# Constant products in TensorE's planned gaps, lower reckoned costs of TensorE, and one PSUM bank for transpositions

## The chip, the cores and the metric

The kernel runs on one core of a Trainium2 chip. The metric is the time of the whole program on the device, in microseconds, and a kernel is judged by the median of several runs. The engines are named as in the profile: PE is TensorE (PEld its weight loads), DVE is VectorE, ACT is ScalarE, POOL is GpSimd and SP is SyncE.

## The reference

Sixteen graphs of 1024 nodes with 64 features each go through four layers. Every layer begins with a layer norm and a ReLU, and its result is added to `x`.

```python
h = jnp.maximum(_layernorm(x, axis=-1), 0.0)
x = x + _L0_gnn_ref(h, adj, L0_gnn_W)     # (adj @ h) @ W.T
...
x = x + _L1_gnn_ref(h, adj, ...)          # two dense layers, adj @ m, a GRU cell
...
x = x + _L2_gnn_ref(h, adj, ...)          # T0 = h, T1 = adj @ h, T2 = 2 adj @ T1 - T0, mixed by K
...
x = x + _L3_gnn_ref(h, adj, nodemask, ...)  # quantiles over thinned lists of neighbours, two dense layers
```

So the first three layers hold four products of a graph's 1024 x 1024 adjacency with 64 columns. The last one lists each node's neighbours, drops some of them by rank, takes three quantiles over the neighbours' rows for every feature, and puts the weighted sum through two dense layers. The adjacency has some nine entries in a row.

## The kernel before

**One program for all graphs.** A graph's nodes lie in 8 tiles of 128. The Python code holds several generators, and each yields one instruction at a time:

- `transposing` loads 128 columns of the adjacency at a time (`block`, 512 KB), transposes them by PE, four 128x128 pieces into one PSUM bank, and lets ACT copy each full bank into half of an `AT` tile. There are 15 `AT` tiles; a graph needs 8 and holds them from its first product with the adjacency to its last.
- `coding` takes the sign of each `AT` tile on ACT (`there`) and multiplies it by powers of two on PE (fp16), so that neighbours are packed in words; `lists` unpacks these on DVE into the neighbours' numbers.
- `layering` runs twice (even and odd graphs) and computes the first three layers in `layers`. Four times per graph a step multiplies the 8 tiles of `h` by the 8 `AT` tiles, two halves of 512 columns each (64 product instructions per graph). Between them are small products by weights, transpositions, and the norms on ACT and DVE. At its end it stores the rows that the last layer gathers (`table`).
- `gathering` waits for a graph's `table` and issues 80 indirect gathers on POOL (10 neighbours of 8 tiles); `quantiling` sorts the gathered rows on DVE by a network of minima and maxima; `dense` sums the weighted places on PE and applies the two dense layers. Nodes with more than 10 neighbours are done once more at the end, in four groups.

**The order.** `Weave` decides the order of all instructions while the program is built. It keeps a reckoned time for each engine. At every step each generator offers its next instruction; the earliest start among the engines wins, and within 0.1 us the lower key (older graph, earlier stage). `Line.cost` (line 309 on) gives each instruction's cost by its engine and shape; `ready` adds 0.15 us for a hand-over between engines. The instructions of one engine are then bound to that order (`behind`), so each engine runs its own queue in order and waits on semaphores for data alone. Costs that are wrong change no result, only the order.

**PSUM.** There are eight banks. Two (`tp`) are for the transpositions of the adjacency, one (`bits`) for coding, two (`q`) for the last layer's dense part and three (`fm`) for the layers. A bank is taken with `yield "tp"` (line 877) and given back after ACT's copy (line 881). Bank 0 is also used by one small product at the end of the program (line 1350).

**The leash.** `issue` can make one engine's instructions wait for another engine's. The two engines are set with `weave.leash`, and they are None and None (line 572): no wait is added.

In the profile nearly all compute instructions carry line 303, that of the helper that records them, so groups are told apart by tiles: `bank<-AT,nodes` is a product with the adjacency, `bank<-c,block` a transposition of it, `bank<-c,there` the coding, `bank<-G,c` the sum over sorted places.

Of the kernel before, what the change touches and what calls it, by code (L numbers as in the profile page):

```python
# [22 lines left out]
P = 128  # L23
# [79 lines left out]
RANK = 3.0  # L103
SHARE = 3
LONGEST = 512
AT = 15
XTILES = 2
PAYS = 3
# [71 lines left out]
def network(n, places, beam=200):  # L180
# [4 lines left out]
    for layer in needed(batcher(n), range(places)):  # L185
        new = {}
        for buf, (cost, ops) in states.items():
            classes = {}
            for a, b, la, lb in layer:
# [73 lines left out]
class Op:  # L263
# [5 lines left out]
    def __init__(self, line, make, writes, reads, cost, later=0.0, after=()):  # L269
        self.line, self.make, self.cost, self.later, self.after = line, make, cost, later, after  # L270
        self.writes, self.reads = [place(a) for a in writes], [place(a) for a in reads]
# [16 lines left out]
class Line:  # L288
# [17 lines left out]
    def cost(self, method, out, reads, kwargs):  # L306
        if method == "dma_start":
            return 0.4, 2.0 + out.nbytes() / 150e3
        n = max(a.free_size() for a in [out] + reads)
        extra = "accum_out" in kwargs  # L310
        if self.name == "DVE":
            fixed = {"match_replace": 0.145, "max": 0.155}.get(method, 0.155)
            return fixed + n / 960 + 0.08 * extra, 0.0
        if self.name == "ACT":
            scalars = sum(hasattr(kwargs.get(k), "ap") for k in ("bias", "scale"))
            return 0.225 + n / 1400 + 0.09 * scalars + 0.19 * extra, 0.0
        if self.name == "PE":
            if method == "transpose":
                return 0.19, 0.25
            n = out.free_size()  # L320
            if n == NB and mybir.dt.size(reads[0].dtype) == 2:
                return 0.075, 0.3
            pair = n == 512 and reads[0].shape[0] == P and out.shape[0] == C
            return (0.58 if pair else max(0.34, 0.06 + n / 545)), 0.3
        return 1.33, 2.2


class Weave:
# [6 lines left out]
    def __init__(self, tc):  # L335
        self.tc = tc
        self.free, self.past, self.last, self.stocks, self.chains = {}, {}, {}, {}, []
        self.ends, self.time, self.free_pairs, self.count = {}, 0.0, set(), 0
        self.leash = None
        self.awaited, self.made = [], {}  # L340

    def stock(self, name, tiles):
        self.stocks[name] = list(tiles)
# [1 line left out]
    def give(self, name, t):  # L345
        self.stocks[name].append(t)
# [10 lines left out]
                        t = max(t, end + (0.0 if line is op.line else 0.15))  # L357
        return t

    def of_others(self, op, line):  # L360

        found = []
        for mine, kinds in ((op.reads, "w"), (op.writes, "wr")):
            for name, lo, hi, p0, p1 in mine:
                for (l, h, q0, q1, kind, other), made in self.made.get(name, {}).items():
                    if other is line and kind in kinds and l < hi and lo < h and q0 < p1 and p0 < q1:
                        found.append(made)
        return [max(found, key=lambda f: f[:2])] if found else []

    def note(self, op, start, ins):  # L370
        end = start + op.cost
        self.count += 1
        for mine, kind in ((op.reads, "r"), (op.writes, "w")):
            for name, lo, hi, p0, p1 in mine:
                past, made = self.past.setdefault(name, {}), self.made.setdefault(name, {})
                if kind == "w":
                    for e in [e for e in past if lo <= e[0] and e[1] <= hi and p0 <= e[2] and e[3] <= p1]:
                        del past[e], made[e]
                past[lo, hi, p0, p1, kind, op.line] = end + op.later
                made[lo, hi, p0, p1, kind, op.line] = end, self.count, ins  # L380

    def advance(self, chain):

# [23 lines left out]

    def issue(self, op, start, of):

        line, ins = op.line, op.make()  # L410
        if line is self.leash[0]:


            done = [i for end, _, i in self.awaited if end <= start]
            self.awaited = self.awaited[len(done):]
            if done:
                self.after(ins, done[-1])
        self.free[line] = start + op.cost
        self.time = max(self.time, start + op.cost)
        if line is not self.leash[1]:  # L420
            self.awaited = sorted(self.awaited + self.of_others(op, self.leash[1]), key=lambda a: a[:2])
        self.note(op, start, ins)
        self.ends[ins.ins.name] = start + op.cost + op.later
        free = False
        for other in self.last.get(line, ()):
            self.behind(ins, other)
        if line in self.last:
            free = (ins.ins.name, self.last[line][0].ins.name) in self.free_pairs
        self.last[line] = [ins] + (self.last[line] if free else [])
        return ins  # L430

    def run(self):
        while True:
            before = None
            while before != (before := [(id(c["want"]), id(c["op"])) for c in self.chains]):
                for chain in sorted(self.chains, key=lambda c: c["key"]):
                    if not self.advance(chain):
                        self.chains.remove(chain)
            heads = [c for c in self.chains if c["op"]]
            if not heads:  # L440
                break
            best = {}
            for c in heads:
                op = c["op"]
                c["start"] = max(self.free.get(op.line, 0.0), op.ready)
                best[op.line] = min(best.get(op.line, 1e9), c["start"])
            line = min(best, key=best.get)
            chain = min((c for c in heads if c["op"].line is line and c["start"] <= best[line] + SLACK),
                        key=lambda c: c["key"])
            op, start = chain["op"], chain["start"]  # L450
            chain["op"], chain["value"] = None, self.issue(op, start, (chain["gen"].__name__, chain["key"]))
        assert not self.chains, [c["want"] for c in self.chains]
# [15 lines left out]
class Fast:  # L468
# [4 lines left out]
    def __init__(self, tc, half, whole, weights):  # L473
        self.tc, self.nc = tc, tc.nc
        (W0, W1, b1, W2, b2, Wih, bih, Whh, bhh, Wc, K, bc, M1, mb1, M2, mb2) = weights
        nc = self.nc
# [7 lines left out]
        _, at16, _, at32 = fast_constants()  # L484
# [84 lines left out]
        self.G, self.D = Line("POOL", nc.gpsimd), Line("SP", nc.sync)  # L569
        self.A = self.S  # L570
        self.take = {}
        weave.leash = None, None

        def stock(name, count, shape, dtype=F32):
            weave.stock(name, [p.tile(shape, dtype, name=f"{name}{i}") for i in range(count)])

        banks = [ps.tile([P, 512], F32, name=f"bank{i}") for i in range(8)]
        self.bank = banks[0]
        weave.stock("tp", banks[0:2])
        weave.stock("bits", banks[2:3])  # L580
        weave.stock("q", banks[3:5])
        weave.stock("fm", banks[5:8])
# [10 lines left out]
        stock("block", 2, [P, NT, P])  # L593
        stock("AT", AT, [P, N])
        stock("X", XTILES, [P, NT, C])
# [183 lines left out]
    def longest(self):  # L779
# [5 lines left out]
        for _ in range(3):  # L785
            tiles.append((yield "AT"))
        run = tiles[0][:, 0:BINS * Q]
# [59 lines left out]
        for t in tiled:  # L847
            self.weave.give("AT", t)


    def transposing(self, adj):
# [17 lines left out]
        for i in range(total):  # L869
# [4 lines left out]
            block = blocks.pop(i)  # L874
            at = yield "AT"
            for half in range(2):
# [39 lines left out]
    def layers(self, w, b, x):  # L916
# [9 lines left out]
        def into(bank, h, last=False):  # L926

            def step(j):
# [6 lines left out]
                if last:  # L935
                    yield lambda: self.masked[b] > j
                    give("AT", turned[j])
            return step
# [208 lines left out]
    def quantiles(self, c):  # L1147
# [21 lines left out]

        few = max(1, int(LONGEST / (T * C)))  # L1170

# [342 lines left out]
def general_layers(tc, b, x, adj, nodemask, VT, mB, X, H, maskT, c16, ident, ones16, ones_row, eps,  # L1514
# [3 lines left out]
    with tc.tile_pool(name="g1", bufs=1) as p1, tc.tile_pool(name="g2", bufs=2) as p2, \  # L1518
# [16 lines left out]
        def neighbours(g):  # L1535
            AT = p2.tile([P, NT, N], F32, name="AT")
            CN = p1.tile([P, NT, N], F16, name="CN")
# [434 lines left out]
```

## Time and profile before

| what | value |
|---|---|
| three runs | 2184.63, 2185.75, 2197.86 us; median 2185.75 |
| profiled execution, its own time | 2165.2 us |
| its span, first to last instruction | 2163.3 us |
| mean granted TensorE clock | 0.785 |
| busy time of PE, DVE, ACT, POOL | 1616.2, 1607.7, 1066.9, 1429.7 us |
| transpositions of the adjacency, mean of one | 345 ns |
| ACT's copies of them (256) | 150.6 us, 591 ns each |
| HBM | 120.12 MB read, 19.17 MB written |

The three layers of all graphs are done after about 1811 us; what is left then is the gathering, sorting and dense part of the last graphs, and the groups of nodes with many neighbours. In the 40 slices of the page a digit is the busy share of an engine in a slice of 54 us, in tenths, and PEclk the clock granted to TensorE in tenths of the full one. In a line of stretches, each engine's busy time is followed by its number of instructions, and the last three numbers are the granted clock, the DMA share and GB/s. A float32 product stands in the records as two matmuls, a transposition as one. PE's matmuls are pipelined, so that their records overlap.

### The profile page before, as it was taken

Reading aid. Unit: us, or ns where it says so; the run is one execution under the profiler, and the core shown is the slowest. Engines: PE = TensorE matmul, PEld = TensorE weight load, DVE = VectorE, ACT = ScalarE, POOL = GpSimd, SP = SyncE. Lnnn points to the kernel's source line nnn. Section 1 sums busy time; section 2 is a strip of 40 time slices with the busy share of each in tenths; the row PEclk is TensorE's granted clock in tenths of the full one; section 3 lists DMA queues with packets and bytes.
Section 4 is the critical chain, followed back from the end, with each engine's and each line's share of the span. In section 5 each row is a group of like instructions: output and inputs, shape, how many; then the busy total and the mean of one; then the engine's idle time right before and its main releaser. Section 6 shows DMA issues by size and latency. Waiting matters only on the chain. (4 is left out here: it accounts for less than half of the span.)

```text
span 2163.3 us, 24623 instructions
## 1 busy us (share of the span) xinstructions
PE 1616.2 (75%) x7024; PEld 745.6 (34%) x7024; DVE 1607.7 (74%) x4253; ACT 1066.9 (49%) x2905; POOL 1429.7 (66%) x1441
## 2 busy tenths in 40 slices
PE   6878787889888987988887978887978865243303
PEld 3433433334333433443433343433334322121302
DVE  1381487787787887869797868787877799959746
ACT  3554655555666456554757475656566632011000
POOL 2027677757576767767576777676767677776772
PEclk9978787797889698869798789889688876555555
DMA  4242525233334234242425242425242213121110
GB/s 120 69 91 47 105 46 95 60 72 77 59 96 66 66 67 95 50 89 56 100 55 100 49 95 61 93 60 105 51 73 70 41 30 43 32 31 22 33 27 11
DMA packets 246846, 141.04 MB, mean 65 GB/s; under 512 B 76048, under 2 KB 223952, under 8 KB 246704
## 3 DMA queue, kind: packets, MB, share of 16 engines
q1 hardware_dynamic: 195664, 88.11, 17.0%
q0 software_dynamic: 46096, 48.62, 14.7%
q10 hardware_dynamic: 4944, 2.67, 0.5%
q8 instruction: 59, 0.97, 0.2%
q14 instruction: 83, 0.68, 0.1%
HBM read 120.12 MB, written 19.17 MB: 64 GB/s over the span
## 5 line engine op out<-in xcount | busy, mean ns | idle before, releaser
L626 POOL DMA_INDIRECT G<-table,pay x1402 | 1400.0, 999 | 687.2 <-issue 358.1
L303 PE MATMUL bank<-AT,nodes 128*64 128x512 f32 x2048 | 588.6, 671 | 87.7 <-ACT nodes L303 73.1
L303 PEld LDWEIGHTS bank<-AT,nodes 128*64 128x64 f32 x2048 | 155.7, 152 | 391.2 <-issue 231.7
L303 PE MATMUL bank<-c,block 128*128 128x128 f32 x976 | 229.4, 345 | 64.8 <-ACT AT L303 40.3
L303 PE MATMUL bank<-G,c 128*128 128x512 f32 (+3 forms) x382 | 175.8, 592 | 130.4 <-DVE G L303 123.0
L303 PEld LDWEIGHTS bank<-c,block 128*128 128x128 f32 x976 | 146.3, 174 | 230.6 <-issue 153.2
L303 ACT ACTIVATE AT<-bank 128x512 f32<-128x512 f32 x256 | 150.6, 591 | 139.9 <-PE bank L303 136.7
L303 DVE TENSOR_TENSOR G<-G 128x512 f32<-128x512 f32 (+3 forms) x313 | 198.3, 677 | 2.3
L303 ACT ACTIVATE wide<-bank 64x512 f32<-64x512 f32 x128 | 75.3, 589 | 164.6 <-PE bank L303 163.4
L303 ACT ACTIVATE sq<-X,st 128x64 f32<-128x64 f32 x360 | 125.4, 348 | 62.0 <-DVE st L303 42.7
L303 ACT ACTIVATE nodes<-X,off,ri 128x64 f32<-128x64 f32 x360 | 143.4, 434 | 23.4 <-DVE off L303 22.6
L303 DVE TENSOR_TENSOR net<-G 128x512 f32<-128x512 f32 (+6 forms) x240 | 151.0, 674 | 4.4 <-ACT G L303 2.7
L303 ACT ACTIVATE G<-G,coef 128x64 f32<-128x64 f32 x384 | 98.9, 341 | 103.2 <-DVE coef L303 103.2
L303 PEld LDWEIGHTS bank<-G,c 128*128 128x128 f32 x382 | 70.1, 227 | 188.9 <-issue 105.8
L303 ACT ACTIVATE there<-AT 128x1024 f16<-128x1024 f32 x128 | 132.3, 1050 | 0.8
L303 PE MATMUL bank<-wide,wg 64*64 64x512 f32 (+1 forms) x192 | 114.7, 687 | 5.9 <-ACT wide L303 5.4
L303 DVE TENSOR_TENSOR G<-net 128x512 f32<-128x512 f32 (+7 forms) x189 | 116.9, 672 | 0.8
L303 DVE TENSOR_TENSOR G<-G,net 128x512 f32<-128x512 f32 (+3 forms) x177 | 110.4, 672 | 0.8
L303 DVE SCALAR_TENSOR_TENSOR G<-bad,G 128x512 f32<-128x512 f32 (+1 forms) x176 | 110.4, 695 | 0.0
L303 DVE RECIPROCAL ri<-sd 128x8 f32<-128x8 f32 x64 | 12.8, 200 | 120.6 <-ACT sd L303 120.4
L303 DVE MAX8 L<-cand 128x8 f16<-128x103 f16 x384 | 92.1, 263 | 8.6
L303 DVE TENSOR_TENSOR net<-G,net 128x512 f32<-128x512 f32 (+3 forms) x140 | 88.2, 670 | 0.1
(199 smaller groups left out, 2359.3 us busy)
## 6 DMA issues: line engine op xcount, KB each, us to landing
block<-in_adj SPq DMA_DIRECT2D x121, 512.0 KB, 4.2
G<-table,pay POOLq DMA_INDIRECT x1402
rows<-pay SPq DMA_DIRECT2D x16, 632.0 KB, 8.8
table<-pay SPq DMA_DIRECT2D x16, 264.0 KB, 4.2
X<-in_x SPq DMA_DIRECT2D x16, 256.0 KB, 8.0
out<-yo SPq DMA_DIRECT2D x16, 256.0 KB, 2.6
G<-in_adj SPq DMA_DIRECT2D x3, 512.0 KB, 9.1
G<-in_adj ACTq DMA_DIRECT2D x3, 512.0 KB, 10.7
```

The source lines that it names most:

```text
L303: return Op(self, lambda: f(*args, **kwargs), writes, reads, cost, later)
L626: return self.nc.gpsimd.indirect_dma_start(out=out, out_offset=None, in_=table, in_offset=bass.IndirectOffsetOnAxis(ap=at, axis=0))
```

## The change

Four things change, in the planner and in the banks.

1. `Line.cost` reckons PE's instructions lower: a transposition 0.125 us (was 0.19), an fp16 product of 64 columns 0.05 (was 0.075), a product with half an `AT` tile 0.27 (was 0.58), any other max(0.15, 0.06 + n/1100) (was max(0.34, 0.06 + n/545)).
2. `fill` is called before every PE instruction. Where the planned start lies more than 0.22 us after the end of PE's last one, and a `layering` generator still lives, it issues products of a constant tile with itself (`ones16`, fp16, 128 rows, 512 columns) into a bank that nobody reads. Their number is such that the planned work of PE in the last 3.4 us comes to half of it, and takes at most 0.7 of the gap. These products have no cost in the plan, and wait for nothing but their place in the queue.
3. Bank 0 becomes the bank of these products. The transpositions keep one bank, `banks[1:2]`.
4. The leash is taken out with its records.

```diff
+WINDOW = 3.4
+DENSITY = 0.5
+SPARE = 0.7
+FILL = 0.22
...
             if method == "transpose":
-                return 0.19, 0.25
+                return 0.125, 0.25
             n = out.free_size()
             if n == NB and mybir.dt.size(reads[0].dtype) == 2:
-                return 0.075, 0.3
+                return 0.05, 0.3
             pair = n == 512 and reads[0].shape[0] == P and out.shape[0] == C
-            return (0.58 if pair else max(0.34, 0.06 + n / 545)), 0.3
+            return (0.27 if pair else max(0.15, 0.06 + n / 1100)), 0.3
...
-        line, ins = op.line, op.make()
-        if line is self.leash[0]:
-
-
-            done = [i for end, _, i in self.awaited if end <= start]
-            self.awaited = self.awaited[len(done):]
-            if done:
-                self.after(ins, done[-1])
+        line = op.line
+        if line is self.filled:
+            self.fill(start, op.cost)
+        ins = op.make()
...
+    def fill(self, start, cost):
+
+        line = self.filled
+        gap = start - self.free.get(line, 0.0)
+        self.recent = [(a, c) for a, c in self.recent if a > start - WINDOW]
+        if gap > FILL and any(c["gen"].__name__ == "layering" for c in self.chains):
+            lacking = DENSITY * WINDOW - sum(c for _, c in self.recent)
+            for _ in range(int(min(lacking, SPARE * gap) / FILL)):
+                ins = self.filler()
+                for other in self.last.get(line, ()):
+                    self.behind(ins, other)
+                self.last[line] = [ins]
+                self.recent.append((start, FILL))
+        self.recent.append((start, cost))
...
-        weave.leash = None, None
+        weave.filled = self.T
...
-        self.bank = banks[0]
-        weave.stock("tp", banks[0:2])
+        self.bank = spare = banks[0]
+        weave.filler = lambda: nc.tensor.matmul(spare, self.ones16[:, 0:P], self.ones16, start=True, stop=True)
+        weave.stock("tp", banks[1:2])
```

More of the change, by code (lines that the diff above doesn't have):

```diff
@@ L337, in __init__ @@
         self.free, self.past, self.last, self.stocks, self.chains = {}, {}, {}, {}, []
-        self.ends, self.time, self.free_pairs, self.count = {}, 0.0, set(), 0
-        self.leash = None
-        self.awaited, self.made = [], {}
+        self.ends, self.time, self.free_pairs = {}, 0.0, set()
+        self.filled, self.recent = None, []
     def stock(self, name, tiles):
@@ L358, in ready, with note @@
         return t
[L360 to L370, printed above, removed]
+    def note(self, op, start):
         end = start + op.cost
-        self.count += 1
         for mine, kind in ((op.reads, "r"), (op.writes, "w")):
             for name, lo, hi, p0, p1 in mine:
-                past, made = self.past.setdefault(name, {}), self.made.setdefault(name, {})
+                past = self.past.setdefault(name, {})
                 if kind == "w":
                     for e in [e for e in past if lo <= e[0] and e[1] <= hi and p0 <= e[2] and e[3] <= p1]:
-                        del past[e], made[e]
+                        del past[e]
                 past[lo, hi, p0, p1, kind, op.line] = end + op.later
-                made[lo, hi, p0, p1, kind, op.line] = end, self.count, ins
     def advance(self, chain):
@@ L408, in issue @@
     def issue(self, op, start, of):
-        line, ins = op.line, op.make()
-        if line is self.leash[0]:
-            done = [i for end, _, i in self.awaited if end <= start]
-            self.awaited = self.awaited[len(done):]
-            if done:
-                self.after(ins, done[-1])
+        line = op.line
+        if line is self.filled:
+            self.fill(start, op.cost)
+        ins = op.make()
         self.free[line] = start + op.cost
         self.time = max(self.time, start + op.cost)
-        if line is not self.leash[1]:
-            self.awaited = sorted(self.awaited + self.of_others(op, self.leash[1]), key=lambda a: a[:2])
-        self.note(op, start, ins)
+        self.note(op, start)
         self.ends[ins.ins.name] = start + op.cost + op.later
```

## The prediction

> **What bounds the kernel now.** I read the page first, then POOL's rows in order of time, then the stretches between one graph's result and the next, then PE's rows in one such stretch.
>
> From the page: engine totals, the granted clock in 40 slices, and the group of gathers.
> ```profile
> PE 1616.2 (75%) x7024; PEld 745.6 (34%) x7024; DVE 1607.7 (74%) x4253; ACT 1066.9 (49%) x2905; POOL 1429.7 (66%) x1441
> ...
> PE   6878787889888987988887978887978865243303
> ...
> PEclk9978787797889698869798789889688876555555
> ...
> L626 POOL DMA_INDIRECT G<-table,pay x1402 | 1400.0, 999 | 687.2 <-issue 358.1
> ```
> No engine is full by this. But a gather takes 0.95 to 1.4 us and POOL needs another 0.30 us ("issue") before the next, so 80 gathers of a graph take 103.9 us on average (100.3 to 107.6, first start to last end of each graph in POOL's rows). The first gather starts at 141.3 us and that of graph 15 at 1819.8: 15 periods of 111.9 us. The 8 us between are POOL waiting for the next graph's table, as in its timeline at the change from graph 6 to graph 7:
> ```profile
> 797.56 0.95 POOL L626 DMA_INDIRECT G<-table,pay  x1 [0.30 <-issue]
> 798.81 0.95 POOL L626 DMA_INDIRECT G<-table,pay  x1 [0.31 <-issue]
> 812.14 0.94 POOL L626 DMA_INDIRECT G<-table,pay  x1 [12.38 <-DVE L L303]
> ```
> The wait is 12.4 us there; all such waits between graphs sum to 121 us. The DVE named is long done: the table of graph 7 was stored at 807.6. So the layers set the period and POOL comes next, 8 us behind. The layers of two graphs hardly overlap: a graph holds its 8 AT tiles from its first aggregation to its last, and there are 15, so the eighth tile of graph b+1 is transposed only when graph b gives its first one back. In the trace graph b+1's first aggregation is added 13 to 22 us after graph b's last. A period is therefore the latency of one graph's chain.
>
> Stretches from one graph's last addition of X to the next one's (length, then busy time and count of PE, PEld, DVE, ACT, POOL, then the clock):
> ```profile
> 340.00:459.50 119.50, 99.36 (x387) 44.59 (x384) 90.34 (x242) 64.92 (x179) 90.30 (x92) 0.74 0.37 72
> 459.50:574.60 115.10, 98.11 (x447) 44.22 (x447) 92.88 (x248) 70.98 (x200) 78.91 (x80) 0.83 0.36 75
> 574.60:684.10 109.50, 94.22 (x416) 41.04 (x415) 89.67 (x242) 67.51 (x189) 74.02 (x76) 0.89 0.35 71
> 684.10:798.90 114.80, 101.16 (x428) 46.46 (x427) 89.20 (x240) 64.96 (x174) 82.98 (x87) 0.78 0.39 80
> ```
> Where the clock is lower, the period is longer. Over the 12 periods from 340 to 1701 us a line through length and clock falls 7.1 us per 0.1 of clock (correlation -0.76). Following the waits back through single periods says the same: PE holds 26 to 27 us of the chain in periods of 108.5 and 109.5 us, and 41 to 69 us in those of 115 to 119.5.
>
> The clock has two values in the records, 1.0 and 0.5, and changes at multiples of 3.41 us; up to 1730 us it is at 0.5 for a third of the time. Two stretches at one value each, and PE's rows there:
> ```profile
> 744.00:762.40 18.40, 18.40 (x58) 10.02 (x56) 11.80 (x23) 5.91 (x10) 13.91 (x15) 0.50 0.22 49
> 784.00:798.90 14.90, 14.59 (x90) 6.61 (x87) 14.78 (x30) 4.26 (x7) 11.24 (x13) 1.00 0.38 62
> ```
> ```profile
> 686.72 0.64 PE L303 MATMUL bank<-c,there 128*128 128x64 f16 x16
> 702.85 0.69 PE L303 MATMUL bank<-c,block 128*128 128x128 f32 x2 [4.58 <-ACT AT L303]
> 713.51 1.97 PE L303 MATMUL bank<-wide,w 64*64 64x512 f32 x2
> 735.44 1.02 PE L303 MATMUL bank<-wide,wg 128*128 128x512 f32 x2
> 785.62 3.65 PE L303 MATMUL bank<-AT,nodes 128*64 128x512 f32 x16 [0.32 <-DVE nodes L303]
> ```
> One f32 product of 512 columns stands as two records: 1.02 us at clock 1.0, 1.97 at 0.5. Eight paired products with AT take 3.65 us at 1.0, 0.46 each. The 4.58 us gap ahead of 702.85 is what the change aims at: behind it PE stays at 0.5 for over 20 us, though it then works nearly without a pause.
>
> **The change, part by part.**
> The leash was set to None, None: it added no wait, so its removal costs nothing and uncovers nothing.
>
> Clock. The new matmuls stand in planned gaps, so that PE is reckoned busy half of any 3.4 us. Real gaps lie only partly where planned ones do, so I take three fifths of the low time as cured: 0.826 becomes about 0.93 in the layers, and by the line above the period falls by 0.104 x 71 = 7.4 us. Ends: 0, if the clock does not rise, and 12.3 (0.174 x 71), if it is 1.0 throughout; beyond 7.7 (111.9 less 104.2: 103.9 and one pause of 0.3) POOL takes over as the bound.
>
> The Trainium skill bears on this ("TensorE: Matmul & The Clock Gate", Part 1: The HAM clock gate): it gives half and full clock and a window of 3.4 us, which agrees with the records here. The same page ("A second HAM failure mode: psum-queue depth-cycling") speaks against the change's one bank: PE that pauses between groups for a bank swings between both clocks. By that rule this part would be 0 and the sum +4 a period, +60 us in all; by the rows it is -7.4 a period.
>
> Fillers. A filler is one f16 product of 512 columns. No such row with 128 rows exists. 16 f16 products of 64 columns, twice as many columns, take 0.64 us at 1.0, so half of that is an upper end, 0.32; the steps inside that run are 29 ns, eight times that is 0.23, the value I take at 1.0, and 0.46 at 0.5. Its number: per graph the new plan reckons 64 x 0.27 + 96 transpositions x 0.125 + 64 x 0.05 + 32 x 0.15 + 8 x 0.18 + 25 x 0.525 + 2 x 0.29 = 52 us of PE (100 us by the old figures), and a plan period is at least 80 x 1.33 = 106 us. PE is thus reckoned 49% busy, and only windows below half are filled: nothing if it were spread evenly, a quarter of the time (27 us) if each window were full or empty. I take 9 us, 40 fillers a graph, some 600 in all. They have no semaphore to wait for; they cost where PE's queue is late and the gap is gone. Behind a filler wait the next product and whatever ACT and DVE do with it. A third on the chain gives +3 us a period; ends 0 and 18 (40 x 0.46, all on the chain). What hides the rest is PE waiting for ACT and DVE.
>
> One bank. A graph has 16 half tiles: four transpositions, then a copy by ACT of 0.59 us (256 copies, 150.6 us). With two banks PE transposes the next half beside the copy; now it starts after it. On the chain is the one tile that graph b+1 lacks, whose second half comes later by about one copy and two handovers, +1 us; ends 0 and 9.4 (16 x 0.59). The other 15 halves have most of a period. The queues behind are PE's, where a transposition that waits for ACT holds the products after it, and ACT's, which has the norm of the layers behind the copy. The DMA of `block` (median landing 4.2 us) waits for the later release, but its tiles lie ahead by up to 7.
>
> Order. PE is now reckoned at 0.27 where the trace has 0.46 at its best, so DVE and ACT get the chain's next step earlier in their queues and wait there, with sorting of gathered rows (0.7 us apiece) held behind them. This favours the chain and takes DVE's slack: DVE is busy 90 of 112 us. I take 0, ends -4 (the shortest full period, 108.1, against 111.9) and +8 (about half of DVE's 22 idle us lost).
>
> Sum per period: -7.4 + 3 + 1 + 0 = -3.4 us; 15 of them -51. Start and tail: up to 141 us the clock is 0.93 already, 0 to -5; from 1924 us on POOL has the last 122 gathers and PE gets no fillers, -5 to +10; I take +2 together. So -49 us on the profiled execution, 2165.2 (span 2163.3) to 2116. The three runs have a median of 2185.75, 0.95% above it; in proportion that makes 2136.
>
> **The rivals.**
> 1. POOL-bound: clock near 1.0, fillers hidden. Every gap of POOL between graphs shrinks to 0.3 us: -7.7 x 15 = -116, 2068 by the runs. For it: periods at 0.89 and 0.84 reach 108 to 109. Against it: in those DVE's queue holds about 50 us of the chain, which no clock shortens.
> 2. Gain and cost cancel: -7.4 against fillers, bank and DVE's waits of 5 to 9 a period; within 22 us, 2164 to 2207. For it: at 702 us the chain waited behind 15 us of list work on DVE, and a faster PE would only wait there.
> 3. Slower: the fillers stand in the way. PE's plan is short by 0.19 us for each of 64 paired products and by 0.3 to 0.5 for each of 25 wide ones, 12 and 10 us a graph, so the queue is late and the gaps filled do not exist. From 32 fillers (7.4 / 0.23) of a graph on the chain this decides; with 40 at 0.46 it is 18.4 + 1 - 7.4 = +12 a period, +180; at two thirds of 40 at a price between (0.35) it is +3, and with the clock not raised +7 to +10. Middle about +4 a period: +60, 2246. Against it: up to 1730 us 31% of PE's time has no column streaming (each record counted for its step at its clock) even now.
> 4. The clock does not rise (a part of 3): from 744.0 to 762.4 us PE is busy 18.40 of 18.40 us and stays at 0.50, so being busy was not enough there.
>
> **How the numbers follow.** About 1% (22 us) is what a measurement of this kernel can tell from no change. Forecast (gain of 25 to 85 us, 2100 to 2161): 0.38. Rival 1: 0.12. Rival 2: 0.20. Rivals 3 and 4: 0.30. Faster 0.50, same 0.20, slower 0.30. The time is 2136. Leaving out some 0.06 below and 0.13 above, the range is 2078 to 2240; the forecast's own is 2100 to 2161.
>
> **What would show it.** Right: clock of 0.9 or more between 141 and 1730 us, some hundreds of f16 rows of 512 columns, waits of POOL between graphs below 6 us, periods near 108. The bank: AT copies waiting longer for PE, PE's transpositions for ACT. Wrong: clock below 0.88; DVE idle over 25 us a period with waits for PE; over 1000 fillers; POOL waiting for DVE's sorting in place of the table.

## The result and the profile after

| kernel | runs | median (lowest to highest) |
|---|---|---|
| before | 4 | 2185.19 us (2180.31 to 2197.86) |
| changed | 4 | 2518.13 us (2514.95 to 2522.38) |

The ratio is 1.1559, 95% interval 1.1505 to 1.1612: slower by 15.6%, far above the range of the prediction. The profiled execution spans 2514.0 us for 2163.3, 351 us more.

From the page of the changed kernel, the engines' busy time, the clock by slices, the gathers, the fillers and ACT's copies of AT:
```profile
PE 1802.2 (72%) x7702; PEld 783.2 (31%) x7702; DVE 1604.9 (64%) x4253; ACT 1079.6 (43%) x2910; POOL 1397.0 (56%) x1441
...
PEclk8997979798988978897788879797878656555555
...
L627 POOL DMA_INDIRECT G<-table,pay x1402 | 1367.7, 976 | 1070.0 <-DVE net L307 468.0
...
L579 PE MATMUL bank<-ones 128*128 128x512 f16 x678 | 243.6, 496 | 0.4 <-DVE wg L548 0.4
L307 ACT ACTIVATE AT<-bank 128x512 f32<-128x512 f32 x256 | 151.2, 591 | 180.3 <-PE bank L307 179.0
```
Apart from PE with its 678 fillers, no engine's busy time grew by more than 1.2%. What grew is idle time: POOL's ahead of its gathers, 687 us before, is 1070, and 468 of it ends with `net`, the tile of the sorting network. Before and after (total, times, longest):
```profile
POOL G L626 <- DVE net L303: 11.7, 3, 11.1
POOL G L627 <- DVE net L307: 468.0, 14, 57.0
```
Here is POOL at the change from one graph to the next (start, length, instruction, idle time before it):
```profile
1343.49 1.04 POOL L627 DMA_INDIRECT G<-table,pay  x1 [0.30 <-issue]
1344.84 0.94 POOL L627 DMA_INDIRECT G<-table,pay  x1 [0.30 <-ACT sq L307]
1363.98 1.14 POOL L627 DMA_INDIRECT G<-table,pay  x1 [18.20 <-DVE net L307]
```
In the kernel before, the gap here (797.56 to 812.14 in the prediction; counted from 0, as below, it is the one ahead of graph 6) ended when the table was there: its store was issued 5 us ahead of the gather. Now the table of this graph (number 9) was stored at 1311.1, 53 us ahead. What the gather waits for is its buffer: there are two `G` buffers, and DVE's sorting of graph 7, which runs from 1275.5 to 1379.0, must have read the places that graph 9's rows overwrite. So the layers' table no longer sets the period; DVE's queue with the sorting in it does, though DVE is busy less than before, 64% for 74%.

How that can be is seen in ten periods, from the first gather of graph 3 to that of graph 13. Columns: the window, its length, busy time and count of PE, PEld, DVE, ACT, POOL, then the clock, DMA share and GB/s. Before:
```profile
472.80:1603.10 1130.30, 972.71 (x4223) 434.52 (x4221) 904.44 (x2431) 678.78 (x1872) 795.66 (x801) 0.83 0.37 75
```
After:
```profile
545.90:1918.00 1372.10, 1121.85 (x4768) 471.99 (x4766) 904.03 (x2431) 701.36 (x1904) 775.35 (x800) 0.84 0.36 61
```
DVE does the same 904 us with the same 2431 instructions. The period went from 113.0 to 137.2 us, and DVE's idle time in it from 22.6 to 46.8: both by 24.2. What DVE waits for most in these windows (total, times, longest), before:
```profile
DVE ri L303 <- ACT sd L303: 81.4, 28, 8.6
DVE st L303 <- DMA X<-in_x: 23.2, 6, 5.6
DVE of_h L303 <- ACT wide L303: 17.5, 10, 3.9
DVE yo L303 <- PE bank L303: 14.9, 10, 6.2
```
After:
```profile
DVE nodes L307 <- ACT G L307: 117.3, 8, 17.4
DVE of_h L307 <- ACT wide L307: 92.7, 11, 10.5
DVE st L307 <- DMA X<-in_x: 49.6, 9, 9.6
DVE yo L307 <- PE bank L307: 49.5, 15, 6.3
DVE X L307 <- PE bank L307: 44.4, 11, 5.8
```
`st` waits for the load of a graph's `x`. The other four are layer or dense instructions with an operand that PE makes: a bank (`nodes`, `yo`, `X`), or a bank and the `wide` that ACT makes of another (`of_h`). The rows of these four sum to 304 us; DVE's idle time in the ten periods grew by 242, and the wait of `ri` fell from 81.4 to 15.1. One such wait, in DVE's timeline:
```profile
1385.91 2.48 DVE L307 TENSOR_TENSOR G<-G,coef 128x512 f32<-128x512 f32 x4
...
1393.55 0.28 DVE L307 TENSOR_TENSOR there<-there,c 128x256 f16<-128x256 f16 x1
1404.88 0.48 DVE L307 SCALAR_TENSOR_TENSOR nodes<-nodes,kc,bank 128x256 f32<-128x256 f32 x1 [11.05 <-ACT G L307]
1405.28 0.33 DVE L307 TENSOR_TENSOR hits<-G,pay 128x160 f32<-128x160 f32 x1
```
And PE's at the same time:
```profile
1392.35 1.94 PE L307 MATMUL bank<-AT,nodes 128*64 128x512 f32 x8 [0.93 <-ACT nodes L307]
...
1397.96 2.80 PE L307 MATMUL bank<-AT,nodes 128*64 128x512 f32 x12
1400.69 1.13 PE L307 MATMUL bank<-G,c 128*128 128x512 f32 x2
1401.75 1.08 PE L307 MATMUL bank<-AT,nodes 128*64 128x512 f32 x4
1403.61 0.46 PE L307 MATMUL bank<-c,wide 64*128 64x64 f32 x4 [0.78 <-ACT wide L307]
1404.32 0.46 PE L307 MATMUL bank<-c,wide 64*128 64x64 f32 x4 [0.25 <-ACT wide L307]
```
`hits`, at 1405.28, is the first instruction of the sorting of graph 8. The last gather of its rows ended on POOL at 1345.8, 59 us earlier. During the first 43 of them DVE still has graph 7 to sort, whose last step there is the row at 1385.91; it ends at 1388.4. For the other 17 us `hits` stands in DVE's queue behind work of other graphs, at the end behind `nodes`, which needs what PE ends at 1404.78 (ACT's `G`, which the row names, is no operand of it). From 1392.35 to 1402.83 PE works through 16 products with AT, 16 of the coding and 2 of the dense part nearly without a pause. At full clock, by the trace's 0.46 us, the 16 products alone are 7.4 us; the plan reckons them at 0.27, 4.3 us. These 3 us are a part of the wait of 11.05 us. What the rest is made of (PE coming late to the products, or the steps behind them) these rows do not show.

The same once more over a whole sorting, from `hits` to the coefficients after it, for graph 8. Before:
```profile
1182.10:1248.40 66.30, 62.81 (x250) 24.78 (x249) 58.27 (x109) 31.66 (x70) 51.97 (x48) 0.79 0.22 45
```
After:
```profile
1405.30:1520.70 115.40, 87.40 (x392) 39.75 (x392) 85.03 (x234) 59.00 (x156) 55.12 (x58) 0.81 0.45 67
```
The 66 us have become 115: 27 us more of other graphs' DVE work stands between (234 instructions in the stretch for 109), and DVE idles 30 us for 8. Over graphs 3 to 12 the mean is 112.6 us for 70.0.

### The profile page after: what moved, and what is told of

Read it like the earlier page. It is cut to its first block, busy times and chain, and to the rows that moved or that the text cites. A ratio compares the mean times of both kernels' runs of the same rounds, so it can differ in the third digit from the quotient of the medians.

```text
span 2514.0 us, 26045 instructions
## 1 busy us (share of the span) xinstructions
PE 1802.2 (72%) x7702; PEld 783.2 (31%) x7702; DVE 1604.9 (64%) x4253; ACT 1079.6 (43%) x2910; POOL 1397.0 (56%) x1441
## 3 DMA queue, kind: packets, MB, share of 16 engines
q8 instruction: 65, 1.06, 0.2%
## 5 line engine op out<-in xcount | busy, mean ns | idle before, releaser
L627 POOL DMA_INDIRECT G<-table,pay x1402 | 1367.7, 976 | 1070.0 <-DVE net L307 468.0
L307 PE MATMUL bank<-AT,nodes 128*64 128x512 f32 x2048 | 608.1, 680 | 96.5 <-ACT nodes L307 83.6
L307 PE MATMUL bank<-G,c 128*128 128x512 f32 (+3 forms) x382 | 193.5, 640 | 275.5 <-DVE G L307 271.9
L307 PE MATMUL bank<-c,block 128*128 128x128 f32 x976 | 216.0, 341 | 131.0 <-ACT AT L307 96.8
L307 PEld LDWEIGHTS bank<-AT,nodes 128*64 128x64 f32 x2048 | 149.0, 151 | 409.0 <-issue 252.0
L579 PE MATMUL bank<-ones 128*128 128x512 f16 x678 | 243.6, 496 | 0.4 <-DVE wg L548 0.4
L307 PEld LDWEIGHTS bank<-c,block 128*128 128x128 f32 x976 | 131.1, 168 | 287.7 <-ACT AT L307 144.1
L307 DVE SCALAR_TENSOR_TENSOR nodes<-nodes,kc,bank 128x256 f32<-128x256 f32 x32 | 15.2, 476 | 166.8 <-ACT G L307 132.0
L307 DVE SCALAR_TENSOR_TENSOR of_h<-bank,bhn,wide 64x512 f32<-64x512 f32 x32 | 23.8, 744 | 146.5 <-ACT wide L307 136.1
L579 PEld LDWEIGHTS <-ones 128*128 128x128 f16 x678 | 77.0, 120 | 111.2 <-issue 86.6
```

Of the source, the lines that this page charges most:

```text
L307: return Op(self, lambda: f(*args, **kwargs), writes, reads, cost, later)
L579: weave.filler = lambda: nc.tensor.matmul(spare, self.ones16[:, 0:P], self.ones16, start=True, stop=True)
L627: return self.nc.gpsimd.indirect_dma_start(out=out, out_offset=None, in_=table, in_offset=bass.IndirectOffsetOnAxis(ap=at, axis=0))
```

## The experiments

Three theories. **A**: the lower costs alone do it, through the order. It has two forms. A1: PE's real time exceeds the reckoned, so that every DVE instruction that needs PE comes up too early in DVE's queue and holds what is behind it. A2: with short reckoned layers the plan runs the layers far ahead and places the sorting late, without slack. **B**: the fillers delay PE. **C**: one bank delays the transpositions.

A number that is needed to read the ratios: on some of the chips ("odd" below) the kernel before itself took 3402 to 3420 us, for 2156 to 2185 on the others ("ordinary"), for a reason that these runs leave open (last section), so a ratio is compared only with those of the same chip or the same kind of chip.

### The parts by themselves

Costs only: the kernel before with the three lines of costs in `Line.cost`.
```diff
-                return 0.19, 0.25
+                return 0.125, 0.25
...
-                return 0.075, 0.3
+                return 0.05, 0.3
...
-            return (0.58 if pair else max(0.34, 0.06 + n / 545)), 0.3
+            return (0.27 if pair else max(0.15, 0.06 + n / 1100)), 0.3
```


> The kernel before with the lower PE costs in the planner alone: two banks for transpositions, no constant products. Theory A (the order made by costs below the real ones: layers are led ahead, DVE waits for PE in their steps, sorting ends late and POOL waits for gathered rows to be freed): most of the loss is here, 2400 to 2500 us, and POOL's waits for DVE net sum to over 300 us. Theory B (the constant products delay the chain): about 2150 or less, a gain. Theory C (one bank: each half tile waits for ACT's copy): about 2150.

Bank only: the kernel before, with
```diff
-        weave.stock("tp", banks[0:2])
+        weave.stock("tp", banks[1:2])
```


> The kernel before with one bank for transpositions alone, old costs, no constant products. Theory A: 2190 to 2230 us. Theory B: the same as A. Theory C: 2400 us or more, with ACT's AT copies and PE's transpositions waiting for one another by over 300 us more in all.

Bank and fillers: the changed kernel with the three cost lines put back.

> The changed kernel with the old PE costs: one bank and constant products in the gaps of the old order. The old order has few gaps (PE is reckoned nearly full), so I expect under 300 constant products. Theory A: 2190 to 2260 us. Theory B: 2300 to 2450. Theory C: like the kernel with one bank alone, 2400 or more. The granted clock of this run against that with one bank alone tells what the constant products do to the clock.

No fillers: the changed kernel with
```diff
-        weave.filled = self.T
+        weave.filled = None
```


> The changed kernel without its constant products: lower costs, one bank. Theory A: 2450 to 2520 us, nearly all of the loss stays. Theory B: 2200 or less. Theory C: 2450 to 2520 as well, told from A by the kernels with one of the two alone.

These four ran on one chip, before at 3405.08 us. Costs only 1.1333 [1.1296, 1.1371]; bank only 1.0157 [1.0108, 1.0205]; bank and fillers 1.0232 [1.0173, 1.029]; no fillers 1.0949 [1.0908, 1.099]. The costs stand out, but the chip was one of the odd ones, so two were run again, on a chip where before takes 2155.63 us.

> The lower PE costs alone once more, beside the kernel before on another chip: in the run before this one the kernel before itself took 3405 us, with 1 to 3 us between small instructions of DVE that took none in the profile of before. Theory A (order): 1.10 to 1.16 of the kernel before, POOL's waits for DVE net over 300 us. Theory B (constant products) and theory C (one bank): 1.00 or less, since neither is in this kernel.

> Lower costs and one bank without constant products, once more. Theory A: 1.10 to 1.16 of the kernel before, at most 2% below the changed kernel's 1.156. Theory B: 1.02 or less. The difference to the kernel with lower costs alone is what one bank does in this order: I expect 0 to 2%.

Costs only 1.1976 [1.1886, 1.2066], no fillers 1.1874 [1.1786, 1.1963]. Both lie above the 1.10 to 1.16 that I gave for A. So the costs alone make all of the loss and more, and B and C fall as its cause. The ten periods of costs only:
```profile
537.80:1993.90 1456.10, 1072.51 (x4304) 443.16 (x4304) 903.47 (x2439) 703.50 (x1919) 780.35 (x801) 0.76 0.31 57
```
And of the kernel without fillers:
```profile
545.10:1958.30 1413.20, 1060.00 (x4325) 456.60 (x4324) 904.02 (x2431) 701.88 (x1904) 772.18 (x801) 0.76 0.33 59
```
145.6 us a period with the costs alone, 141.3 with one bank besides, 137.2 with the fillers too (that one on another chip, on which before was 1.4% slower). Single periods are uneven, so the choice of ten matters: over all fifteen, from the first gather of graph 0 to that of graph 15, they are 140.6, 138.4 and 135.7, for 111.9 before. The fillers are thus worth 3 to 4 us a period here: the clock of these windows is 0.76 without them and 0.84 with them. On two odd chips the same pair, 1.0949 without (above) and 1.0897 with them (below), is not told apart.

Bank only and bank with fillers were repeated too, and fell on a chip of the odd kind (before 3419.65 us).

> One bank for transpositions alone, old costs. 1.00 to 1.02 of the kernel before: the other chip had 1.016, and in the order of the lower costs one bank cost nothing (1.187 with it, 1.198 without).

> One bank and constant products with old costs: how many products the old order takes, what they do to the clock, and what that is worth. If the clock is worth what the line through the periods said, a rise by 0.03 gives 1% against the kernel with one bank alone; if constant products mostly delay the chain, it is slower than that kernel. I expect 0.99 to 1.02 of the kernel before.

1.0142 [1.0105, 1.0178] and 1.019 [1.0153, 1.0228]: as the first time. In the old order one bank costs 1.4 to 1.6% on these chips, and fillers save nothing there: 264 of them, as few as expected, raise the clock of the whole run only from 0.668 to 0.681 in the first pair of profiles. On an ordinary chip neither was measured in the old order.

### Distance or place

One-pass products: costs only, and the products with AT read the upper halves of their operands as bf16. This changes the computation (coarser sums over neighbours). In the repeat on an ordinary chip the 1024 products then keep PE busy for 253.9 us, 0.25 each, for 645.5 us, 0.63 each, with the costs alone: PE's real time comes to the reckoned 0.27.
```diff
-                    yield T.matmul(bank[half * C:(half + 1) * C, :], h[:, j, :], turned[j][:, cols[half]],
+                    yield T.matmul(bank[half * C:(half + 1) * C, :], h[:, j, :].bitcast(BF16)[:, 1::2],
+                                   turned[j][:, cols[half]].bitcast(BF16)[:, 1::2],
```


> Lower costs alone, and the four products with the adjacency per graph take the upper 16 bits of their float32 operands as bf16, so that one product of 512 columns is one pass and not four: the arithmetic is coarser, the instructions and their order are the same. Theory A in the form A1 (the loss is the distance between reckoned and real times of PE: DVE and ACT wait in the layers' steps): a paired product takes some 0.11 us a column half at full clock, below the 0.27 reckoned, and the time falls from 1.19 to 0.95-1.05 of the kernel before. Form A2 (the order itself is bad: sorting placed late, whatever PE does): stays above 1.10.

Sorting first: costs only, and in `quantiling` a lower key, which wins ties within 0.1 us of planned start against the layers of later graphs.
```diff
-            yield c["key"]
+            yield c["key"] - 1.0
```


> Lower costs alone, and the key of quantiling lowered by 1, so that sorting of a graph stands equal with the layers of the graph three later and ahead of listing. Form A2 (sorting is held behind other work in DVE's queue): the sorting stretch from hits to coef falls from over 100 us to under 90, and the time to 1.05 or less. Form A1: the waits of DVE for PE stay, and the time stays at 1.12 to 1.20.

On a chip of the odd kind (before 3419.65): 1.0613 [1.0567, 1.0658] and 1.0885 [1.0838, 1.0932], for 1.1333 of costs only. Both help, and both lie in neither form's range. They were repeated, with two that change only the size of the costs.

> The kernel before with the new costs, and the four adjacency products of each half tile read the upper 16 bits of their operands as bf16 (one pass in place of four), so that TensorE's real time comes down to the reckoned 0.27 us; the values of the aggregation are coarser for it. Costs alone gave 1.198 on an ordinary chip, 1.133 on one with sparse VectorE instructions, where this edit brought 1.061. A1 (real time longer than reckoned): 1.00 to 1.06. A2 (sorting planned late): products are not what it waits for, 1.12 to 1.19.

> The kernel before with the new costs, and the chain that sorts gathered rows takes the lower key (its own key less one), so that it goes ahead of the layers of the graphs behind it. It brought 1.089 for 1.133 on a chip with sparse VectorE instructions. A2: 1.00 to 1.08, POOL's wait for the sorting network under 250 us in all (550 with costs alone). A1: 1.14 to 1.20, since the sorting is still in a queue behind products that come late.

Costs as measured: the kernel before with PE's costs as its own trace has them at full clock.
```diff
-                return 0.19, 0.25
+                return 0.11, 0.25
...
-                return 0.075, 0.3
+                return 0.03, 0.3
...
-            return (0.58 if pair else max(0.34, 0.06 + n / 545)), 0.3
+            return (0.43 if pair else max(0.22, 0.06 + n / 600)), 0.3
```


> The kernel before with TensorE's costs as its own trace has them at clock 1.0: transposition 0.11, pair 0.43, f16 0.03, the smallest 0.22, n/600. The planned total is 2082 us, as with the new costs (2061), so POOL bounds the plan here too and the layers are planned to be early; but the distance of reckoned from real time at full clock is gone. A1: 1.00 to 1.06. A2: 1.10 to 1.18, as the plan leaves the sorting as little slack.

Pair cost only: 0.27 for 0.58, the rest as before.

> The kernel before with one cost changed: a paired product at 0.27 for 0.58 (64 a graph, 20 of the 48 us of TensorE's time that the new costs take out of a graph). Planned total 2066 us, as low as with all the new costs. A1: the loss in proportion to the time left out, 20/48 of 20%, 1.06 to 1.10. A2: the plan is POOL-bound as with all of them, 1.14 to 1.20.

These four ran on an ordinary chip (before 2155.97). One-pass products 1.0573 [1.0517, 1.0629]; sorting first 1.1222 [1.1164, 1.128]; costs as measured 1.0828 [1.0767, 1.0889]; pair cost 1.0645 [1.0584, 1.0705]. Ten periods of one-pass products:
```profile
465.30:1699.30 1234.00, 851.52 (x3635) 405.42 (x3634) 903.73 (x2439) 698.85 (x1913) 783.08 (x800) 0.69 0.34 67
```
Of sorting first:
```profile
524.40:1828.60 1304.20, 989.14 (x4267) 457.85 (x4268) 907.19 (x2436) 699.85 (x1915) 780.01 (x800) 0.76 0.33 64
```
Of costs as measured:
```profile
517.10:1753.70 1236.60, 1001.30 (x4385) 449.33 (x4386) 903.41 (x2431) 701.02 (x1921) 783.89 (x800) 0.81 0.35 68
```
Of pair cost only:
```profile
511.70:1714.20 1202.50, 1010.97 (x4406) 455.89 (x4406) 905.95 (x2440) 714.87 (x1937) 798.03 (x801) 0.81 0.36 70
```
DVE's work is 903 to 907 us in each ten periods, so the period is 90.4 us and DVE's idle time. Set beside the PE time that the planner reckons for a graph (its own sum over transposing, coding, layers and dense part; by hand, without some small products, the prediction has 100 and 52):

| kernel | reckoned PE, us a graph | period | DVE idle in it | ratio |
|---|---|---|---|---|
| before | 101.6 | 113.0 | 22.6 | 1 |
| pair cost only | 81.8 | 120.2 | 29.7 | 1.064 |
| costs as measured | 74.4 | 123.7 | 33.3 | 1.083 |
| costs only | 53.3 | 145.6 | 55.3 | 1.198 |
| ... and sorting first | 53.3 | 130.4 | 39.7 | 1.122 |
| ... and one-pass products | 53.3 | 123.4 | 33.0 | 1.057 |

The less PE is reckoned, the longer DVE idles: 7, 11 and 33 us for 20, 27 and 48 us left out. Shorter real products by the same reckoning give back 22 of the 33 us. That is A1, and the pair cost alone lies in its range too (1.06 to 1.10). But 22 us is not all, sorting first gives back 16 without touching PE's time, and the costs as measured miss A1's range (1.00 to 1.06) as they miss A2's. POOL's wait for `net` goes the same way: 11.7 us in all before, 213.0, 273.2 and 549.7 as more PE time is left out, 286.9 with one-pass products.

Sorting first is no clean win for A2 either. The mean stretch from `hits` to the coefficients (graphs 3 to 12) falls from 118 us with the costs alone to 83, as A2 said, but the ratio lies in neither form's range and POOL still waits 371.9 us for `net`, not under 250. So both forms have a part. How large each is stays open: 28 of the 48 us left out are not pair products, so what one-pass products do not give back can be distance as well as place.

The old pair cost, 0.58, is above what the product takes at full clock; over the clock of these windows it is about right, an estimate of 0.46 / 0.83 = 0.55. Before, the row of these products has 588.6 us for 1024 of them, 0.57 each. That is why "as measured" at full clock still reckons PE too fast.

Two doubts remained: whether one-pass products are faster by the old costs too, so that their ratio has the wrong base, and whether the order can be mended from either side.

> The kernel before, by its old costs, with the four adjacency products of each half tile reading the upper 16 bits of their operands as bf16 (values of the aggregation coarser). It is the base for the one-pass kernel by the new costs (1.057). If products hold the chain by the old order: 0.94 to 0.97, and the one-pass kernel by the new costs loses 9 to 12% against its own base. If the old order leaves no gain to a faster product, since its queues are fixed: 0.98 to 1.01.

> The changed kernel with the lower key for the chain that sorts gathered rows (its own key less one). A2 (sorting planned late carries the loss): 1.00 to 1.06. A1 (mostly the distance of the reckoned times): the same two fifths of the loss as by the costs alone, 1.08 to 1.12.

> The kernel before with TensorE's costs a tenth above the old ones (transposition 0.21, f16 0.08, pair 0.64, smallest 0.38, n/500): between the real time at full and at half clock. If the distance alone counted, 0.98 to 1.00. If the old costs fitted the chip (their planned total was 2161 for a span of 2163), no gain, 1.00 to 1.03, with the layers planned later and POOL waiting for its table.

> The changed kernel beside the others of this call, on the same chip: 1.15 to 1.17.

The chip was of the odd kind (before 3401.96). Old costs with one-pass products 0.982 [0.9755, 0.9885]: hardly faster, as expected of queues that are fixed by the order. On such chips the one-pass kernel by the new costs is thus 1.0613 / 0.982 = 1.081 of its own base, for 1.133 with float32 products: two fifths of the loss go there, not half. The changed kernel again 1.0897 [1.0827, 1.0966], below the 1.15 to 1.17 expected, which came from an ordinary chip; with sorting first 1.0529 [1.0465, 1.0592]: 41% of the loss, for 34% (odd) and 38% (ordinary) by the costs alone, though the number lies in the range I gave for A2. Costs a tenth above the old ones 1.0178 [1.0101, 1.0256] (transposition 0.21, fp16 0.08, pair 0.64, smallest 0.38, n/500): no gain on that side either.

Settled: the costs make the loss, and on an ordinary chip all of it, in the ten periods, is idle time of DVE. Not settled: the shares of distance and place, on an ordinary chip above all, where the one-pass kernel has no base of its own. No version tried beats the kernel before.

## Why the prediction was wrong

**What bounds the kernel** was read rightly: the layers' chain, POOL 8 us behind, DVE with 22 us of slack. What I did not ask of the third is what uses that slack up.

**Order**, the step that failed: "This favours the chain and takes DVE's slack ... I take 0, ends -4 (the shortest full period, 108.1, against 111.9) and +8 (about half of DVE's 22 idle us lost)". The mechanism is in it: DVE gets its next step too early and waits, with the sorting behind. The size is not: costs only measured +32.6 us a period (145.6 less 113.0), four times the upper end. I bounded the loss by the idle time that DVE had, as if DVE could lose at most that before it became the bound. But the waits of its in-order queue did not come out of the 22.6 us; they were added to the period, and the idle time grew to 55.3. The prediction had already the numbers for it: PE was reckoned 52 us a graph for 100 by the old figures, 64 x 0.19 and 25 x 0.3 to 0.5 us short even at full clock. Rival 3 used those 22 us to say when gaps for fillers vanish; I did not carry them into DVE's waits. It also counted the chain only: the layers did run ahead (table stored 53 us early), and the bound went to the other end, the sorting that holds `G`. I named that as a sign of being wrong ("POOL waiting for DVE's sorting in place of the table"), and that sign came, with two more: DVE idle over 25 us a period (46.8) and the clock below 0.88.

**Clock**: -7.4 and a rise to 0.93. Against before the clock hardly rose (0.84 for 0.82 up to 1800 and 1730 us). Against the same order without fillers it did, 0.76 to 0.84, and as 0.84 is below 0.88 the step is wrong by its own test. The lower costs had taken from the clock what the fillers gave back: with the costs alone PE is busy 74% of the ten periods, 86% before, at 0.76 for 0.83. What a rise is worth in the old order is not shown either: with 264 fillers no gain came (odd chips). The line of 7.1 us per 0.1 was weaker than I put it; with the period before the twelve (107.7 us at 0.79) its slope is 5.6 and its correlation -0.57.

**Fillers**: number and price were about right, 678 for some 600, and 0.23 and 0.46 us foretold. In the trace a filler follows the one before by 216 ns at clock 1.0 and 427 at 0.5. The Trainium skill ("TensorE: Matmul & The Clock Gate", Part 1, Wait — 56ns, not 53.3ns?) gives 215.7 and 426.7 ns for 512 columns; the trace agrees. My net of clock and fillers was -4.4 us a period (-7.4 + 3); without fillers against with them it is -4.1 (141.3 to 137.2, across two chips), or -2.7 over all fifteen periods. That it is so near is in part luck: the period was set by something else than in my sum, and how much of the fillers lies on a chain was not measured.

**One bank**: +1, ends 0 and 9.4. In the old order 1.4 to 1.6% on the odd chips (some 50 us, 3 a period); in the new order a gain on either kind, 1.133 to 1.095 on an odd chip, 145.6 to 141.3 us a period on an ordinary one (140.6 to 138.4 over all fifteen), whose cause was not sought. The waits that I foretold came: by the same costs, with two banks and with one, ACT's copies wait 144.2 and 194.9 us for PE, PE's products and transpositions 36.0 and 142.7 us for these copies. In this order they did not lengthen the period. The rule that I cited against one bank ("A second HAM failure mode: psum-queue depth-cycling" of the same page) does not show: by the same costs the mean clock is 0.729 with two banks and 0.728 with one. The page tells of a kernel that cycles through banks, and that it would hold for one bank was my inference.

**Sum**: +32.6 - 4.3 - 4.1 = +24.2 us a period for the -3.4 foretold; over all fifteen periods +28.7 - 2.2 - 2.7 = +23.8. The terms are differences between kernels on different chips, on which before differed by 1.4%, so that each is good to some 2 us. The net of clock and fillers was foretold within that and one bank was off by 3 to 5; the step taken as 0 decided. **Rivals**: 3 and 4 had the right sign, and the clock did not rise against before, as 4 has it, but neither names the cause; 2246 was still 270 us short. **Range**: its upper end came from fillers on the chain, so it could not hold a loss by order.

## What to carry to other kernels

Where a plan fixes in-order queues, a cost is a promise to every other queue. Reckoned too low, as here, it brings consumers up early, and each waits with unrelated work behind it. Price such an edit by the time left out (in this kernel a third to two thirds of it came back as the period's growth), not by the slack of the engine that waits. And read costs at the clock that the stage is granted, not at the full one.

## What the runs showed of the hardware

On chips where the kernel before takes 3400 us, the records have idle time ahead of some short instructions of DVE that they do not have on the others. The group of MAX8 in the lists' unpacking, in the changed kernel on an ordinary chip:
```profile
L307 DVE MAX8 L<-cand 128x8 f16<-128x103 f16 x384 | 92.9, 263 | 8.4
```
And the same kernel on an odd chip:
```profile
L307 DVE MAX8 L<-cand 128x8 f16<-128x103 f16 x384 | 92.9, 263 | 98.0 <-remote 76.0 <-issue 12.5 <-DVE cand L307 1.4
```
One takes 263 ns on both. The idle time ahead of them is 8 and 98 us, on the odd chip in 41 gaps, most of 1.1 to 3.2 us; with one bank only, on an odd chip too, it is 244 us. "remote" is a wait whose end the profile puts down to another core or an unknown queue. PE too has idle time there that no recorded event ends: 142.4 us ahead of the products with AT are "issue", where the ordinary chip has none. What makes it was not found. The loss by the new costs is smaller on such chips, 1.133 for 1.198.
